# First norms with tokens on partitions and spread through a diagonal, constant products ahead of them, division and second root moved

## The chip, the cores and the metric

The kernel runs on 1 core of one Trainium2 chip. The metric is the device time of one execution in microseconds (us), lower is better. Runs of the kernel before took 2447.05, 2449.82 and 2451.08 us; the median is 2449.82 us.

The core has five engines with queues of their own, each in order: TensorE (PE; its weight loads are shown apart as PEld), VectorE (DVE), ScalarE (ACT), GpSimd (POOL) and SyncE (SP). In this kernel SP's queue issues most transfers, and POOL's queue issues those that add to what lies at their target.

## What is computed

One conditioned transformer block, with x added once more. Everything is float32.

```python
def _tc_rmsnorm(x, t, gw, gb, bw, bb):
    g = (t @ gw.T + gb)[:, None, :]
    b = (t @ bw.T + bb)[:, None, :]
    inv_rms = jax.lax.rsqrt(jnp.mean(x * x, axis=-1, keepdims=True) + EPS)
    return g * x * inv_rms + b

def _attention(x, Wq, Wk, Wv, Wo):
    ...
    attn = jnp.einsum('blhd,bmhd->bhlm', q, k) / scale
    p = jax.nn.softmax(attn, axis=-1)
    o = jnp.einsum('bhlm,bmhd->blhd', p, v).reshape(B, L, D)
    return o @ Wo.T

def _swiglu(x, gate_w, hid_w, out_w):
    return jax.nn.silu(x @ gate_w.T) * (x @ hid_w.T) @ out_w.T

y = x + _attention(_tc_rmsnorm(x, t, g1w, g1b, b1w, b1b), Wq, Wk, Wv, Wo)
y = y + _swiglu(_tc_rmsnorm(y, t, g2w, g2b, b2w, b2b), gate_w, hid_w, out_w)
return x + y
```

x is 4 x 1024 x 512, the condition t 4 x 128; there are 16 heads of 32, and the hidden width is 2048. EPS is 1e-6.

## The kernel before

**Layout and tiles.** Features lie on the 128 partitions, tokens along the free dimension: a tile of x is 128 x 4 x 512 (4 chunks of features, 512 tokens, a "block"). There are 8 blocks, two for each batch. The mean over features in a norm is therefore a product with a matrix `ones_mean` of 1/512 on PE, which also spreads the mean over all partitions.

**Start (L707 to L738).** The tiles y[0, 0] and y[0, 1] of the first batch are loaded and normed ahead of the loop. `norm_sum` (L210) squares four chunks on ACT, adds them up by four products with `ones_mean`, takes the root on ACT (L218) and the reciprocal on DVE (L219), both on 128 x 512. `norm_rest` (L222) scales each chunk on DVE (L199) and applies g and b on ACT (L202). `modulation` (L718) computes g and b by 16 narrow products (L722). Then come the first projections to keys, queries and values.

**The loop (L774).** One step g is one round of attention scores for 4 heads, 256 queries and 256 keys. Four steps make a group j (kind = g % 4 is the place in it), 32 steps make a block of tokens, and there are 256 rounds. A step computes `scores` on PE and copies them out on ACT (`keep`, L323); `running_max` follows on DVE; one group later `shifted` (L369) subtracts the maximum on DVE, ACT takes the exponential (L372), and `weighted` (L382) multiplies by v on PE a step after that. `accumulate` (L396) adds up the exponentials by transfers from POOL's queue, and `fold_sum`, `sums` and `sums_out` bring a group's sum of exponentials to the tile `total`, three groups after its scores, at kind 0. `inverse` (L422) and `normalize` (L431) divide the group's output by it on DVE: a reciprocal and a product on 128 x 256. Between `max_T` (L337) and `shifted`, the maximum goes through `parts` (DVE), `parts_T` (L353, transposes on PE into a PSUM tile pt at kind 1), a copy mT on ACT and two products `spread` (tiles sp) that ACT copies to `shift`.

**The feed-forward part.** From step FS = 60 on (`ffn`), the steps also carry the feed-forward products of the block before: an even and the following odd step share one p, a piece of 128 hidden features. The four half products use the tiles pa (`bank_a`) and pb; `filler` (L746) multiplies earlier pieces with the output weights into a tile pc, and `take_contract` (L583, "evict") adds pc to `res` on DVE. For p below 4 the filler is a late projection of values instead, and its eviction a copy on ACT. On an even step the order is: pair_26, copy_156, sums (kind 0), exponential, max_T and parts (kind 0), filler, running_max, evict, pair_7, sub_5 (L552), and at the end of the step the division of group j_n, where `in_first` places it at kind 0 or kind 2. On an odd step: pair_3, gate_tanh, exponential, pair_15 (next pa), take_5, then the gates.

**Order.** PE, DVE, ACT and POOL run in exactly the order in which the program issues instructions (`manual_schedule`, L704); work is hung on steps by four tables: `pinned` (near the start), `amid`, `halfway` and `ended` (the end of the step; `after` fills it). SP's transfers follow in their order too.

**PSUM.** Eight banks: four for scores (`ps_sc`), one for `av`, two of tag "w" in pool `ps`, one in `ps_b`. In the feed-forward stretch pb holds `ps_b`; pa, pc, pt, sp and the sums use tag "w". A tile waits for a bank until the last reader of an earlier tile there is done.

**Second norms (L648 to L676).** For block n, with e near the block's end: `norm_squares`, `norm_mean` (e + 17; product and a copy on ACT, L157), `norm_compact` writes one row of 512 means to DRAM, `take` reads it back as 128 x 4 (e + 19), `root` takes the root on ACT (e + 20, L173), `invert` the reciprocal on DVE (e + 21, L177), `put` writes it to DRAM (e + 22, L182), and `norm_spread` reads it back to all partitions (e + 24, one transfer, L188). For the first block the last three come one or two steps earlier. The norms of the later batches' inputs (`norm_root`, L149) stay on ACT and DVE with 128 x 512.

Of the kernel before, what the change touches and what calls it, by code (L numbers as in the profile page):

```python
# [9 lines left out]

F32 = mybir.dt.float32
BF16 = mybir.dt.bfloat16
AF = mybir.ActivationFunctionType
ALU = mybir.AluOpType
# [3 lines left out]
P = 128  # L18
NB = 512
# [5 lines left out]
def tile_cond_transformer_block(  # L25
# [13 lines left out]
    nc = tc.nc  # L39
    NBLK, _, C, _ = x.shape  # L40
    B = cond_t.shape[1]
    D = C * P
# [3 lines left out]
    KT = L // P  # L46
# [11 lines left out]
    sb = ctx.enter_context(tc.tile_pool(name="sb", bufs=1))  # L58
# [61 lines left out]
    state = {}  # L120
# [30 lines left out]
    def norm_mean(tag: str, inside: bool):  # L151
        if inside:
            pm = ps_av.tile([P, NB], F32, tag="av", name=f"pm{tag}")
        else:
            pm = ps.tile([P, NB], F32, tag="w", name=f"pm{tag}")
        mm(pm, ones_mean, state[tag], True, True)
        nc.scalar.copy(state[tag], pm)  # L157

    def compact(tag: str, t, rows: int, n: int):

# [3 lines left out]
    def take(tag: str):  # L164

        src = inv_s.pop(tag)
        few = sb.tile([P, src.shape[0] * src.shape[1] // P], F32, tag="few", name=f"few{tag}", bufs=2)
# [3 lines left out]
    def root(tag: str):  # L171
        few = state["few", tag]
        nc.scalar.activation(few, few, AF.Sqrt, bias=eps)  # L173

    def invert(tag: str):
        few = state["few", tag]
        nc.vector.reciprocal(few, few)  # L177

    def put(tag: str):
        few = state.pop(("few", tag))  # L180
# [28 lines left out]

    def norm_sum(dst, tag: str):  # L210

        pm = ps.tile([P, NB], F32, tag="w", name=f"pm{tag}")
        for c in range(C):
            sq = sb.tile([P, NB], F32, tag="h", name=f"sq{tag}_{c}", bufs=7)
            nc.scalar.activation(sq, dst[:, c, :], AF.Square)
            nc.tensor.matmul(pm, ones_mean, sq, start=(c == 0), stop=(c == C - 1))
        inv = sb.tile([P, NB], F32, tag="rmax" if tag == "a0_0" else "tot", name=f"inv{tag}", bufs=1)
        nc.scalar.activation(inv, pm, AF.Sqrt, bias=eps)  # L218
        nc.vector.reciprocal(inv, inv)  # L219
        state[tag] = inv  # L220

    def norm_rest(which: int, b: int, dst, tag: str):  # L222
        for c in range(C):
            norm_scale(dst, tag, c)
            norm_mod(which, b, dst, c)
# [99 lines left out]
    def running_max(r: int, k: int):  # L325
        j, u = divmod(r, UN)
        if u:
            nc.vector.tensor_tensor(rmax[j], rmax[j], raw[r][:, k, :, :], ALU.max)  # L328
        elif k:
            rmax[j] = sb.tile([P, HG, HQ], F32, tag="rmax", name=f"rmax{j}")  # L330
            nc.vector.tensor_tensor(rmax[j], raw[r][:, 0, :, :], raw[r][:, 1, :, :], ALU.max)
# [89 lines left out]
    def inverse(j: int):  # L421
        nc.vector.reciprocal(state["total", j], state["total", j])  # L422
# [183 lines left out]
    def after(g, fn, *a):  # L606
        ended.setdefault(g, []).append((fn, a))
# [40 lines left out]
    for n in range(NBLK):  # L648
        g0 = (n + 1) * BS
        pin(g0 + 6, load_res, n)  # L650
        e = g0 if n == 0 else g0 - 4
        go = e + 13 if n < NBLK - 1 else g0 + 8
        for d in range(C):
            first.append((go, None, project_out, (n, d)))
            pin(go - 3 + (d // 2 * 4 if n else 0), load_wo, n, d)
        if n < NBLK - 1:
            tag = f"f{n}"
            after(e + 16, add_res, n)
            for k in range(2):
                after(e + 15 + k, lambda n=n, tag=tag, k=k: norm_squares(x2[n], tag, k))  # L660
            if n == 0:
                between(e + 17, norm_mean, tag, False)
            else:
                amid.setdefault(e + 17, []).append((norm_mean, (tag, True)))
            after(e + 17, norm_compact, tag)
            after(e + 19, take, tag)
            after(e + 20, root, tag)
            after(e + (20 if n == 0 else 21), invert, tag)
            after(e + (21 if n == 0 else 22), put, tag)
            after(e + (22 if n == 0 else 24), norm_spread, tag)  # L670
            scales, mods = ((24, 24, 25, 25), (25, 25, 26, 26)) if n == 0 else ((22, 22, 24, 24), (23, 23, 25, 25))
# [32 lines left out]
    with tc.manual_schedule(  # L704
# [8 lines left out]
        load_modw(1)  # L713
        fetch()
        fetch()
        norm_sum(y[0, 0], "a0_0")

        def modulation(k: int):  # L718
            pm = ps.tile([P, 4 * C, B], F32, tag="w", name=f"pmod{k}")
            cols = slice(k * 2 * C, (k + 1) * 2 * C)  # L720
            for i in range(k * 2 * C, (k + 1) * 2 * C):
                nc.tensor.matmul(pm[:, i, :], modw[:, i * P : (i + 1) * P], condT, start=True, stop=True)  # L722
            nc.vector.tensor_tensor(
                mod[:, cols, :], pm[:, cols, :], modb[:, cols].unsqueeze(2).to_broadcast([P, 2 * C, B]), ALU.add
            )

        modulation(0)
        norm_rest(0, 0, y[0, 0], "a0_0")
        evicts = [project_kq(0, 0, which, 0) for which in range(2)]
        norm_sum(y[0, 1], "a0_1")  # L730
        for evict in evicts:
            evict()
        norm_rest(0, 0, y[0, 1], "a0_1")
        for kt in range(KT // 2):
            project_v(0, kt)()
            if kt == 0:
                modulation(1)
        project_kq(0, 0, 0, 1)()  # L738

# [34 lines left out]
        while g < END:  # L774
# [40 lines left out]
                keep(g)  # L815
            if kind == 1 and s_on:
                take_av(j_s)
            due = bool(first) and first[0][0] <= g
            if not ffn:
                if x_on:  # L820
# [24 lines left out]
            elif even:  # L845
# [13 lines left out]
                if g < NR:  # L859
                    running_max(g, 0)  # L860
                    running_max(g, 1)
                if evict is not None:
                    evict()
                pair_7(p)
# [3 lines left out]
            else:  # L868
# [143 lines left out]
```

## Time and profile before

| | |
|---|---|
| profiled execution | 2455.29 us |
| its span, first to last instruction | 2453.4 us |
| median of the runs | 2449.82 us |
| DVE / ACT / POOL busy | 1940.7 / 1413.2 / 172.4 us |
| mean granted clock of TensorE | 0.994 |
| L422 DVE reciprocal of total, 128x256 | x64, 1744 ns |
| L431 DVE product with it, 128x256 | x64, 425 ns |
| L583 DVE eviction of pc, 128x512 | x128, 689 ns |
| L173 ACT root, 128x4 | x7, 297 ns, with 7 table loads of 1283 ns |
| L177 DVE reciprocal, 128x4 | x7, 168 ns |
| L219 DVE reciprocal, 128x512 | x2, 3353 ns |
| PE waiting for L372 (exponential) ahead of L382 | 35.1 us, 37 times |

A line of the timeline reads: start in us, duration of the group in us, engine, line of the program, operation, target <- sources, shapes, count; in brackets the idle time of that engine ahead of it and what ended it. Groups of equal neighbours are merged, and matmuls overlap, so that a group of 16 can end after the next has begun. The granted clock (PEclk) is the share of TensorE's clock that was let through.

### The profile page before, as it was taken

How to read it: one execution, taken by the hardware profiler on the slowest of the kernel's cores; microseconds unless marked ns; L12 is line 12 of the kernel's file. 1: busy time of each engine (PE TensorE's matmuls, PEld its weight loads, DVE VectorE, ACT ScalarE, POOL GpSimd, SP SyncE). 2: the span in 40 equal slices, each digit the busy share in tenths (PEclk: the TensorE clock that was granted, in tenths of full speed). 3: DMA queues.
4: the chain of work that ended last, by engine and by line, in shares of the span. 5: the costliest groups of instructions: out<-in, count | busy, mean ns of one | idle time of the engine just before them, and what ended most of it. 6: DMA issues, size and time to landing. Idle time of an engine off the chain costs nothing. (4 is left out here: it accounts for less than half of the span.)

```text
span 2453.4 us, 72677 instructions
## 1 busy us (share of the span) xinstructions
PE 2385.5 (97%) x32553; PEld 1135.9 (46%) x32553; DVE 1940.7 (79%) x2183; ACT 1413.2 (58%) x1495; POOL 172.4 (7%) x207
## 2 busy tenths in 40 slices
PE   8999999999999999999999999999999999999999
PEld 3333334344444544544454544454445445444444
DVE  2688888878799988998899979997999799843332
ACT  3677776765566656665566656665666566512110
POOL 0000000000000000000000000000000000000000
PEclk9999999999999999999999999999999999999999
DMA  6599999988788788889888888898788888853442
GB/s 216 166 304 259 256 258 240 231 202 219 198 205 210 188 226 209 208 207 229 204 200 213 225 197 209 204 230 207 198 207 203 224 200 204 198 165 117 140 131 70
DMA packets 185988, 501.79 MB, mean 205 GB/s; under 512 B 21319, under 2 KB 78663, under 8 KB 158286
## 3 DMA queue, kind: packets, MB, share of 16 engines
q0 software_dynamic: 28656, 208.68, 43.9%
q1 hardware_dynamic: 156734, 288.47, 35.4%
q8 instruction: 256, 4.19, 0.7%
q14 instruction: 54, 0.44, 0.1%
q10 hardware_dynamic: 288, 0.01, 0.0%
HBM read 246.44 MB, written 41.97 MB: 118 GB/s over the span
## 5 line engine op out<-in xcount | busy, mean ns | idle before, releaser
L369 DVE TENSOR_TENSOR raw<-raw,shift 128x2048 f32<-128x2048 f32 (+1 forms) x320 | 588.8, 1857 | 25.6 <-ACT shift L364 25.6
L323 ACT COPY raw<-sc 128x2048 f32<-128x2048 f32 x256 | 479.7, 1874 | 187.4 <-PE sc L316 130.8
L372 ACT ACTIVATE raw<-raw 128x2048 f32<-128x2048 f32 x256 | 490.8, 1917 | 157.1 <-DVE raw L369 154.8
L328 DVE TENSOR_TENSOR rmax<-rmax,raw 128x1024 f32<-128x1024 f32 x384 | 469.5, 1223 | 48.8 <-ACT raw L323 42.2
L112 PE MATMUL pc<-h,ow 128*32 128x512 f32 x4096 | 470.5, 596 | 5.2 <-DMA ow<-in_out_w 4.2
L382 PE MATMUL av<-raw,v 128*32 128x256 f32 x4096 | 271.9, 383 | 35.6 <-ACT raw L372 35.1
L396 POOL DMA_DIRECT2D raw<-raw x192 | 165.3, 861 | 1967.4 <-ACT raw L372 878.9
L316 PE MATMUL sc<-q,k 32*128 32x256 f32 x4096 | 293.3, 400 | 1.0 <-ACT raw L323 1.0
L112 PE MATMUL pa<-x,fa 128*32 128x256 f32 x4096 | 272.5, 384 | 4.1 <-DVE pa L530 4.1
L112 PE MATMUL pa<-sums,fw 128*32 128x256 f32 x4096 | 271.5, 383 | 0.0
L112 PEld LDWEIGHTS pc<-h,ow 128*32 128x32 f32 x4096 | 128.6, 110 | 250.7 <-issue 231.9
L316 PEld LDWEIGHTS sc<-q,k 32*128 32x128 f32 x4096 | 184.9, 184 | 117.4 <-issue 75.8
L112 PE MATMUL pkq<-y,wkq 128*32 128x512 f32 (+1 forms) x1664 | 232.5, 594 | 4.3 <-ACT y L202 4.1
L112 PEld LDWEIGHTS pa<-x,fa 128*32 128x32 f32 x4096 | 124.7, 110 | 119.7 <-DVE pa L530 21.4
L382 PEld LDWEIGHTS av<-raw,v 128*32 128x32 f32 x4096 | 110.4, 109 | 149.4 <-ACT raw L372 66.0
L112 PEld LDWEIGHTS pa<-sums,fw 128*32 128x32 f32 x4096 | 134.4, 111 | 90.0 <-issue 3.4
L583 DVE SCALAR_TENSOR_TENSOR res<-pc,res 128x512 f32<-128x512 f32 x128 | 88.2, 689 | 78.9 <-PE pc L112 76.2
L545 ACT COPY pb<-pa 128x256 f32<-128x256 f32 x128 | 46.1, 360 | 174.4 <-PE pa L112 173.3
L562 ACT ACTIVATE t<-pa 128x512 f32<-128x512 f32 x128 | 78.1, 610 | 109.9 <-PE pa L112 109.6
L112 PE MATMUL pb<-x,fw 128*32 128x256 f32 x2048 | 134.0, 379 | 1.2 <-ACT pb L545 1.2
L112 PE MATMUL pa<-x,fw 128*32 128x256 f32 x2048 | 134.0, 379 | 0.0
L552 DVE TENSOR_TENSOR pb<-pb,p 128x256 f32<-128x256 f32 x128 | 55.0, 430 | 99.8 <-PE pb L112 94.2
(108 smaller groups left out, 2243.7 us busy)
## 6 DMA issues: line engine op xcount, KB each, us to landing
raw<-raw POOLq DMA_DIRECT2D x192, 1024.0 KB, 9.3
fw<-sw SPq DMA_DIRECT2D x128, 512.0 KB, 7.8
fa<-in_gh_w SPq DMA_DIRECT2D x128, 384.0 KB, 6.8
ow<-in_out_w SPq DMA_DIRECT2D x128, 256.0 KB, 3.1
wkq<-in_kq_w SPq DMA_DIRECT2D x32, 512.0 KB, 6.2
v<-vs SPq DMA_DIRECT2D x128, 128.0 KB, 6.6
k<-kqs SPq DMA_DIRECT2D x124, 128.0 KB, 6.5
kqs<-st SPq DMA_DIRECT2D x61, 256.0 KB, 8.3
```

The source lines that it names most:

```text
L112: nc.tensor.matmul(dst[k : k + n, :], w[:, k : k + n], moving, start=start, stop=stop, skip_group_check=seeded)
L316: nc.tensor.matmul(sc[:, i, k, :], keys[rows, k * P : (k + 1) * P], queries[rows, :], start=True, stop=True)
L323: nc.scalar.copy(raw[r].rearrange("p k h q -> p h k q"), state.pop(("sc", r)))
L328: nc.vector.tensor_tensor(rmax[j], rmax[j], raw[r][:, k, :, :], ALU.max)
L369: nc.vector.tensor_tensor(t, t, s.unsqueeze(1).to_broadcast(list(t.shape)), ALU.add)
L372: nc.scalar.activation(raw[r], raw[r], AF.Exp)
L382: nc.tensor.matmul(av[j][i * DH : (i + 1) * DH, :], v[m, u][:, k, i * DH : (i + 1) * DH], raw[r][:, k, i, :], start=(kt == 0), stop=(kt == ...
L396: nc.gpsimd.dma_start(out=acc[j].rearrange("p k h q -> p (k h q)"), in_=raw[r].rearrange("p k h q -> p (k h q)"), accum_op=ALU.add,)
L545: nc.scalar.copy(bank_b[p][:, RIGHT], bank_a[p][:, RIGHT])
L552: nc.vector.tensor_tensor(b[:, LEFT], b[:, RIGHT], fifth.pop(p), ALU.subtract)
L562: nc.scalar.activation(state["t", p], bank_a[p], AF.Tanh, scale=0.5)
L583: nc.vector.scalar_tensor_tensor(r, pp, 0.5, r, ALU.mult, ALU.add)
```

## The change

Four things are changed.

1. `norm_sum`, used twice at the start, adds the four squares on DVE, multiplies each 128 tokens of the sum (as weights) with one column of `ones_mean`, so that tokens lie on partitions, and takes root and reciprocal on 128 x 4. A diagonal 128 x 4 x 128 of these numbers, times 512, is built on DVE, and a later product of `ones_mean` with it spreads them over the partitions into a PSUM tile, from which the scaling reads. That product, `spread_root`, comes after `modulation(0)` for the first norm and after the first projection of values for the second; `modulation(1)` moves one projection later.
2. Eight products of `ones_mean` with itself stand ahead of the first norm.
3. In the second norms the mean gets eps on the way out of PSUM; root and reciprocal are replaced by `inverse_root`: one instruction on DVE that makes a first guess from the bits, and 17 on POOL (four Newton steps), at e + 21. For the first block `put` and `norm_spread` come one step later.
4. In the feed-forward stretch the division of a group moves from the end of the step to just ahead of the eviction. Before step 60 it stays at the end.

```diff
@@ norm_mean @@
-        nc.scalar.copy(state[tag], pm)
+        nc.scalar.activation(state[tag], pm, AF.Identity, bias=eps)
@@ root, invert @@
-        nc.scalar.activation(few, few, AF.Sqrt, bias=eps)
...
-        nc.vector.reciprocal(few, few)
+    def inverse_root(tag: str):
+        few = state["few", tag]
+        y, t = (sb.tile(list(few.shape), F32, tag=f"few{i}", name=f"few{i}{tag}") for i in range(2))
+        nc.vector.tensor_scalar(
+            y.bitcast(I32), few.bitcast(I32), 1, 0x3FFFFFFF, ALU.logical_shift_right, ALU.bitwise_xor
+        )
+        nc.gpsimd.tensor_scalar_mul(y, y, 1.35 * 2.0**62)
+        for _ in range(4):
+            nc.gpsimd.tensor_tensor(t, y, y, ALU.mult)
+            nc.gpsimd.tensor_tensor(t, t, few, ALU.mult)
+            nc.gpsimd.tensor_scalar(t, t, -0.5, 1.5, ALU.mult, ALU.add)
+            nc.gpsimd.tensor_tensor(y, y, t, ALU.mult)
+        state["few", tag] = y
@@ norm_sum @@
-        pm = ps.tile([P, NB], F32, tag="w", name=f"pm{tag}")
+        sq = [sb.tile([P, NB], F32, tag="h", name=f"sq{tag}_{c}", bufs=7) for c in range(C)]
         for c in range(C):
-            sq = sb.tile([P, NB], F32, tag="h", name=f"sq{tag}_{c}", bufs=7)
-            nc.scalar.activation(sq, dst[:, c, :], AF.Square)
-            nc.tensor.matmul(pm, ones_mean, sq, start=(c == 0), stop=(c == C - 1))
-        inv = sb.tile([P, NB], F32, tag="rmax" if tag == "a0_0" else "tot", name=f"inv{tag}", bufs=1)
-        nc.scalar.activation(inv, pm, AF.Sqrt, bias=eps)
-        nc.vector.reciprocal(inv, inv)
-        state[tag] = inv
+            nc.scalar.activation(sq[c], dst[:, c, :], AF.Square)
+            if c:
+                nc.vector.tensor_tensor(sq[0], sq[0], sq[c], ALU.add)
+        nt = NB // P
+        pm = ps.tile([P, nt], F32, tag="w", name=f"pm{tag}")
+        for t in range(nt):
+            nc.tensor.matmul(pm[:, t : t + 1], sq[0][:, t * P : (t + 1) * P], ones_mean[:, 0:1], start=True, stop=True)
+        few = sb.tile([P, nt], F32, tag="few", name=f"few{tag}")
+        nc.scalar.activation(few, pm, AF.Sqrt, bias=eps)
+        nc.vector.reciprocal(few, few)
+        diagonal = sb.tile([P, nt, P], F32, tag="t", name=f"diagonal{tag}", bufs=2)
+        nc.vector.scalar_tensor_tensor(
+            diagonal,
+            ident.unsqueeze(1).to_broadcast([P, nt, P]),
+            float(D),
+            few.unsqueeze(2).to_broadcast([P, nt, P]),
+            ALU.mult,
+            ALU.mult,
+        )
+
+        def spread_root():
+            inv = ps.tile([P, NB], F32, tag="w", name=f"inv{tag}")
+            nc.tensor.matmul(inv, ones_mean, diagonal.rearrange("p t q -> p (t q)"), start=True, stop=True)
+            state[tag] = inv
+
+        return spread_root
@@ second norms of a block @@
-            after(e + 20, root, tag)
-            after(e + (20 if n == 0 else 21), invert, tag)
-            after(e + (21 if n == 0 else 22), put, tag)
-            after(e + (22 if n == 0 else 24), norm_spread, tag)
+            after(e + 21, inverse_root, tag)
+            after(e + 22, put, tag)
+            after(e + (23 if n == 0 else 24), norm_spread, tag)
@@ start @@
-        norm_sum(y[0, 0], "a0_0")
+        ahead = ps.tile([P, P], F32, tag="w", name="ahead")
+        for _ in range(8):
+            nc.tensor.matmul(ahead, ones_mean, ones_mean, start=True, stop=True)
+        spread_root = norm_sum(y[0, 0], "a0_0")
...
         modulation(0)
+        spread_root()
         norm_rest(0, 0, y[0, 0], "a0_0")
         evicts = [project_kq(0, 0, which, 0) for which in range(2)]
-        norm_sum(y[0, 1], "a0_1")
+        spread_root = norm_sum(y[0, 1], "a0_1")
         for evict in evicts:
             evict()
+        project_v(0, 0)()
+        spread_root()
         norm_rest(0, 0, y[0, 1], "a0_1")
-        for kt in range(KT // 2):
+        for kt in range(1, KT // 2):
             project_v(0, kt)()
-            if kt == 0:
+            if kt == 1:
                 modulation(1)
@@ loop, even step of the feed-forward stretch @@
                 if g < NR:
                     running_max(g, 0)
                     running_max(g, 1)
+                divide()
                 if evict is not None:
                     evict()
                 pair_7(p)
@@ loop, end of a step @@
-            if n_on and j_n < direct and kind in (0, 2):
-                at = g - kind
-                in_first = j_n % GB == GB - 1 or (at >= FS and at % BS not in (12, 24, 28))
-                if in_first == (kind == 0):
-                    inverse(j_n)
-                    if j_n != GB:
-                        normalize(j_n)
+            if not ffn:
+                divide()
```

`divide` holds the same condition and the same two calls as the lines that are taken out at the end of the step. The tile `few` of `take` has one buffer instead of two.

More of the change, by code (lines that the diff above doesn't have):

```diff
@@ L11 @@
 F32 = mybir.dt.float32
+I32 = mybir.dt.int32
 BF16 = mybir.dt.bfloat16
@@ L166, in take @@
         src = inv_s.pop(tag)
-        few = sb.tile([P, src.shape[0] * src.shape[1] // P], F32, tag="few", name=f"few{tag}", bufs=2)
+        few = sb.tile([P, src.shape[0] * src.shape[1] // P], F32, tag="few", name=f"few{tag}")
         nc.sync.dma_start(out=few, in_=src.rearrange("h (p c) -> (h p) c", c=few.shape[1]))
         state["few", tag] = few
-    def root(tag: str):
+    def inverse_root(tag: str):
         few = state["few", tag]
-        nc.scalar.activation(few, few, AF.Sqrt, bias=eps)
-    def invert(tag: str):
-        few = state["few", tag]
-        nc.vector.reciprocal(few, few)
+        y, t = (sb.tile(list(few.shape), F32, tag=f"few{i}", name=f"few{i}{tag}") for i in range(2))
[9 more added lines that the diff above has]
+        state["few", tag] = y
     def put(tag: str):
@@ L817, in tile_cond_transformer_block, with divide @@
                 take_av(j_s)
+            def divide():
+                if n_on and j_n < direct and kind in (0, 2):
+                    at = g - kind
+                    in_first = j_n % GB == GB - 1 or (at >= FS and at % BS not in (12, 24, 28))
+                    if in_first == (kind == 0):
+                        inverse(j_n)
+                        if j_n != GB:
+                            normalize(j_n)
             due = bool(first) and first[0][0] <= g
```

## The prediction

> **What bounds the kernel now.** First the page's row of engines, then the waits, then timelines around each place that the diff touches.
>
> ```profile
> PE 2385.5 (97%) x32553; PEld 1135.9 (46%) x32553; DVE 1940.7 (79%) x2183; ACT 1413.2 (58%) x1495; POOL 172.4 (7%) x207
> ```
>
> TensorE is busy for 2385.5 of 2453.4 us: whatever makes it wait is paid nearly in full, and the other engines matter by what they make it wait for. Only 68 us of PE idleness are there to be won, and 5.49 of them lie ahead of its first product.
>
> The second view is the end of a step of kind 0 in the feed-forward stretch, on VectorE and then on TensorE.
>
> ```profile
> 706.84 1.22 DVE L331 TENSOR_TENSOR rmax<-raw 128x1024 f32<-128x1024 f32 x1
> 708.16 0.69 DVE L583 SCALAR_TENSOR_TENSOR res<-pc,res 128x512 f32<-128x512 f32 x1
> 709.09 0.43 DVE L552 TENSOR_TENSOR pb<-pb,p 128x256 f32<-128x256 f32 x1 [0.24 <-PE pb L112]
> 709.43 1.74 DVE L422 RECIPROCAL total<-total 128x256 f32<-128x256 f32 x1
> 711.21 0.43 DVE L431 TENSOR_TENSOR oT<-avs,total 128x256 f32<-128x256 f32 x1
> 711.55 2.35 DVE L369 TENSOR_TENSOR raw<-raw,shift 128x1024 f32<-128x1024 f32 x2
> ```
> ```profile
> 704.45 3.64 PE L112 MATMUL pc<-h,ow 128*32 128x512 f32 x32
> 707.91 1.05 PE L112 MATMUL pb<-x,fw 128*32 128x256 f32 x16
> 708.90 0.27 PE L353 MATMUL pt<-ident_bf,split 128*32 128x128 bf16 x2
> 709.10 1.15 PE L316 MATMUL sc<-q,k 32*128 32x256 f32 x16
> ```
>
> The eviction L583 ends at 708.85 and the transposes pt start at 708.90. This is no accident. The pool `ps` has two banks of tag "w". In this stretch one holds pa(p) until the gate in the next step; the sums, pc, pt, both sp and the next pa take turns in the other. So pt can't start until L583 has emptied pc's bank, and scores, spread and all that follows stand behind pt on PE. I looked at every step of kind 0 after which a division now comes: pt starts 0.05 us after that eviction's end in all of them (739.95 after 739.89, 863.07 after 863.02). That margin is nil.
>
> Third, ScalarE and TensorE two steps later.
>
> ```profile
> 706.92 1.28 ACT L173 ACT_TABLE_LOAD   x1
> 708.22 0.30 ACT L173 ACTIVATE fewf<-fewf,eps 128x4 f32<-128x4 f32 x1
> ...
> 714.42 1.28 ACT L372 ACT_TABLE_LOAD   x1
> ```
> ```profile
> 717.68 1.07 PE L382 MATMUL av<-raw,v 128*32 128x256 f32 x16 [1.39 <-ACT raw L372]
> ```
>
> The small root L173 costs two table loads, and the second delays the exponential that PE then waits for.
>
> **The division moved (50 times, in the feed-forward stretch alone).** Reciprocal 1.74 plus product 0.43 are 2.17 us that now stand ahead of the eviction. The rule of `in_first` puts the division at kind 0 where the group's place in its 32 steps is 0, 4, 8, 16 or 20, else at kind 2.
>
> Kind 0: L331 ends at 708.06, so the eviction would start at 710.23 instead of 708.16: 2.07 later. pt follows it, and so do scores, mT, spread and shift; VectorE, done with its division, waits for the shift. Nothing downstream had slack that this uses up, so I count it whole. At places 4, 8 and 20 VectorE idled 0.41 us for pc ahead of L583, which the division fills: 2.17 - 0.41 = 1.76. There are 11 groups at 0 and 16 (22.8 us), 17 at 4, 8 and 20 (five or six of each; some idle less, 1.77 on average, 30.1 us) and a last one at step 256, without a running maximum, at 0.95. Step 64 is free (ScalarE evicts there), step 68 too (PE waits 4.2 us for ow, longer than the division). Sum **+53.8**. Bounds: 0, if pt had a bank of its own, which the 0.05 us speak against, and 29 x 2.17 = 63.
>
> Kind 2: no transposes follow, and pa comes 2.4 to 2.9 us after the eviction. At place 26 alone it is 1.83, so pa slips by 0.47, ahead of a wait of 1.57 that swallows it. Elsewhere the division fills idle gaps of 0.10 and 0.24 around L583, so that the next shift, exponential and weighted product come 0.34 earlier; twelve waits of PE of 0.27 and 0.20 lie there. I take 12 x 0.34 = **-4** (bounds 0 and -6).
>
> **The clock.** A PE that waits can lose clock. After six equal waits of 1.57 us at place 28, the granted clock was 0.50 for 3.41 us four times, as here, and 1.00 twice:
>
> ```profile
> core 0: us, PE busy (x), PEclk, DMA share, GB/s
> 793.57:796.98 3.41, 3.41 (x36) 0.50 1.08 316
> 1312.40:1315.80 3.40, 2.96 (x44) 1.00 1.10 294
> ```
>
> After waits of 1.39 it never was. That step took 13.65 us against 12.60 without, so one costs 1.05; the most is half of 3.41, 1.71. I cut the trace's matmul starts into windows of 3.41 us: the half-clock stretches inside the kernel follow windows in which nothing streamed for 1.9 us or more. With the new waits put in, and averaged over the phase, some 19 windows are such, against 5 now. 14 more at 1.4 are **+20** (bounds 0 and 29 x 1.71 = 50).
>
> The Trainium skill (TensorE: Matmul & The Clock Gate, section HAM oscillation) names idle gaps above about 3.4 us as what throttles. By that rule the new waits would cost no clock, and the sum would end 20 us lower; the 1.57 us waits of this trace disagree with it, and the rows decide.
>
> **The second norms' root (seven times).** Gone from ScalarE: two loads of 1.28 and a root of 0.30; from VectorE a reciprocal of 0.17. The waits of PE behind them are 1.39 six times and 1.45 once (at 480.78): **-9.8** (bounds 0 and -7 x 2.86 = -20). Added: one VectorE instruction on 128x4 (0.17, as that reciprocal) and 17 on GpSimd. No row has GpSimd arithmetic that small; its memset of 128x1 took 0.10, its select of 128x128 0.28, so 1.7 to 4.8 in all; I take 3. GpSimd idled 12.37 us ahead of its accumulating transfer at 724.41, which hides most of it; that transfer may come 1 us late, in a chain that the fold reads several steps later. `put` on SP's queue then waits until some 723 instead of 720.0. Behind it stand v (720.43), the spread and ow (723.97), read three, two and two steps later, at 5.5 to 10 us a step: cost 0. For the first block `put` and its spread move by one step; the scaling then follows one step of 10.6 us after the spread: 0 as well. Were the cover gone, 7 x 4.8 = 34 at worst. The copy with eps as a bias costs as L149 does, 0.69 for 0.62, on an engine that is 58% busy: 0.
>
> The Trainium skill (ScalarE: Activation LUTs, section What ACT_TABLE_LOAD costs) adds a drain to each load, 2.66 us a switch. By that figure ScalarE would win 7 x 5.6 = 39 us, and were all of it on PE's path the sum would be 29 lower; the rows show 1.28 with no gap around it, and 1.39 on PE.
>
> **The first norms.** Now:
>
> ```profile
> 5.49 5.17 PE L216 MATMUL pma<-sqa,ones_mean 128*128 128x512 f32 x8 [5.49 <-ACT sqa L215]
> 10.51 1.84 PE L722 MATMUL pmod<-condT,modw 128*128 128x4 f32 x16
> 16.41 1.22 PE L112 MATMUL pkq<-y,wkq 128*128 128x512 f32 x1 [4.05 <-ACT y L202]
> ```
>
> A root (0.69) and a reciprocal (3.35) on 128x512 lie ahead of the scaling. After: squares end at 7.67; the last of three sums (0.69) at 8.4; eight narrow passes (1.84 / 16 = 0.115 each) 0.9; root 0.30; reciprocal 0.17; diagonal 0.69 (as L567); with hand-overs 11.1. But pmod stands ahead of the spreading product on PE until 12.35. Then two passes (0.43 each, 0.85 at half clock), a scaling of 0.69, a modulation of 0.82: the projections start at 14.9 to 15.8 instead of 16.41. I take -1.2. In the second norm eight passes of 0.43 and a wait of 0.78 go; eight of 0.115 and two of 0.43 come: -2.4. Together **-3.6**. The eight constant products, 16 passes of 0.11 to 0.21, lie in PE's first 5.49 us, where it waits for x: 0, and 3.4 if they ran into the sums. What they do to the clock is open: it was at 0.52 from 16.41 to 22.35, worth 2.9 us, which may go or come twice. Bounds of the part: -7 and +2.
>
> **Sum.** 53.8 - 4 + 20 - 9.8 - 3.6 = +56.4. The profiled execution took 2455.29 (span 2453.4), 5.5 above the median of the runs, 2449.82; the sum on it is 2511.7, on the median **2506**.
>
> **Rivals.** (1) The wait without the clock: nothing throttles, since the new waits differ from that at place 28 in what surrounds them. Then +36, 2486; against it stand four cases in six. (2) The clock drops at nearly every wait: 53.8 + 50 - 17.4 = +86, 2536. For it: transposes, scores and spread, which use the array thinly, surround each new wait. (3) Faster: pt finds an empty bank, because the slots are given out otherwise than I read them. Then only the gains are left, -17.4, and the filled gaps at kind 0 give nothing, as the shift sets that end: 2432. It decides where pt starts before L583 ends; each pair shown above speaks against it. (4) The wait holds, but VectorE's lead from the early division comes back in the same group: about half of 53.8 stays, with 10 of clock, +20, 2470. Against: pt delays the shift, which VectorE needs next.
>
> **How the numbers follow.** Forecast 0.62, (1) 0.12, (2) 0.08, (4) 0.08, (3) 0.08, and 0.02 that gains and waits cancel. A measurement here tells about 0.2% (5 us) from no change. Slower: 0.90; within: 0.02; faster: 0.08. The range, 2474 to 2536, takes in (1), (2) at its end and most of the bounds of the unknowns; (3) and part of (4) lie below it.
>
> **What would show it.** The transposes L353 with a wait of 1.7 to 2.1 us put down to VectorE in five groups of each block of 32 steps, pt 0.05 after L583, and L583 directly behind L431. Some 20 stretches of half clock, a mean clock near 0.985 instead of 0.994. No table load beside an exponential in the feed-forward stretch, and no 1.39 left. Step 0's scores at 46 to 48 us instead of 50.54. I am wrong if pt starts unhindered, if the gaps close without a change of the span, or if SP's queue, held by `put`, makes PE wait for ow.

## The result and the profile after

The changed kernel took 2518.15, 2518.72, 2522.99 and 2527.08 us, median 2520.85; the kernel before, on the same chip, 2450.45 (2449.82 without one execution of 3478.25 us that stands outside the ratio). The ratio, over the runs and not of the medians, is 1.0296 with a 95% interval of 1.0268 to 1.0324: slower, and inside the predicted range of 2474 to 2536, 15 us above the predicted 2506. The profiled execution is the one of 2518.15 (span 2516.4, mean clock 0.996), against 2455.29 (span 2453.4, clock 0.994) before: 63.0 us more of span.

First the page's row of engines, then the waits of TensorE (line waited on, what released it, us in total, times, longest).

```profile
PE 2393.3 (95%) x32573; PEld 1139.7 (45%) x32573; DVE 1936.3 (77%) x2191; ACT 1393.3 (55%) x1474; POOL 265.9 (11%) x326
```
```profile
PE pt L381 <- DVE res L611: 48.1, 29, 1.9
PE av L410 <- ACT raw L400: 27.5, 32, 1.6
PE pb L113 <- ACT pb L573: 21.2, 7, 4.8
```

TensorE is busy for only 7.8 us more than before, so most of the 63 is waiting. The first wait is new, 29 times, and is the one that the prediction is built on. The third stood at 1.2 us, once, before; now it is 21.2 in seven. And POOL is busy for 265.9 us where it was 172.4: 93.5 more, for 119 instructions that had been put at 0.10 to 0.28 each, 12 to 33 in all.

The place of each microsecond comes from a comparison of the two traces: the start of the scores of every step before and after, and the growth of each step, added up over blocks 2 to 7 by the step's place in its 32 (place 0 to 31).

| Where | Growth, us | What is there |
|---|---|---|
| up to step 0 | -2.1 | first norms (48.47 instead of 50.54) |
| blocks 0 and 1 | -1.6 | a table load's wait gone (1.45) |
| places 0, 8, 16, 20 | +9.2, +9.7, +8.9, +9.7 | wait of pt |
| place 4 | +2.8 | five steps longer by 1.62, for waits of pt of 1.57; the sixth, without a wait of pt, 5.3 shorter: its wait for ow is 2.5 shorter, with less half clock behind it |
| places 1 and 17 | +4.8 | half clock behind a wait of pt |
| place 18 | -8.5 | waits behind a table load gone |
| places 22, 23, 24 | +26.5, +4.4, +4.1 | wait of pb |
| places 27 and 28 | +2.2, -6.4 | four half-clock stretches of before gone |
| tail, after the last scores | -1.0 | |

The rows add up to 62.7. Two causes make nearly all of it: some 45 us for the transposes, where 53.8 and some clock were predicted, and 35 us in steps 22 to 24, which the prediction costed at nothing.

**The wait of pt** on VectorE and TensorE of the changed kernel (start, duration, engine, line, operation, target and sources; idle time before in brackets).

```profile
729.86 1.22 DVE L359 TENSOR_TENSOR rmax<-raw 128x1024 f32<-128x1024 f32 x1
731.00 1.74 DVE L450 RECIPROCAL total<-total 128x256 f32<-128x256 f32 x1
732.78 0.42 DVE L459 TENSOR_TENSOR oT<-avs,total 128x256 f32<-128x256 f32 x1
733.12 0.68 DVE L611 SCALAR_TENSOR_TENSOR res<-pc,res 128x512 f32<-128x512 f32 x1
733.72 0.42 DVE L580 TENSOR_TENSOR pb<-pb,p 128x256 f32<-128x256 f32 x1
```
```profile
727.78 3.64 PE L113 MATMUL pc<-h,ow 128*32 128x512 f32 x32
731.24 1.05 PE L113 MATMUL pb<-x,fw 128*32 128x256 f32 x16
733.85 0.27 PE L381 MATMUL pt<-ident_bf,split 128*32 128x128 bf16 x2 [1.57 <-DVE res L611]
734.06 1.15 PE L344 MATMUL sc<-q,k 32*128 32x256 f32 x16
```

The eviction (now L611) stands directly behind the division and ends at 733.80; pt starts at 733.85, again 0.05 later. Its wait is 1.57 at places 4, 8 and 20 (17 times), 1.88 at 0 and 16 (11 times) and 0.74 in the last group.

**The chain on GpSimd**, and VectorE beside it.

```profile
703.03 0.86 POOL L424 DMA_DIRECT2D raw<-raw  x1 [8.30 <-DMA raw<-raw]
712.37 2.18 POOL L179 TENSOR_SCALAR few0f<-few0f 128x4 f32<-128x4 f32 x1 [8.47 <-DVE few0f L176]
714.63 1.03 POOL L181 TENSOR_TENSOR few1f<-few0f 128x4 f32<-128x4 f32 x1
715.74 1.19 POOL L182 TENSOR_TENSOR few1f<-few1f,fewf 128x4 f32<-128x4 f32 x1
717.01 0.20 POOL L183 TENSOR_SCALAR few1f<-few1f 128x4 f32<-128x4 f32 x1
717.29 0.20 POOL L184 TENSOR_TENSOR few0f<-few0f,few1f 128x4 f32<-128x4 f32 x1
717.57 0.20 POOL L181 TENSOR_TENSOR few1f<-few0f 128x4 f32<-128x4 f32 x1
717.84 2.21 POOL L182 TENSOR_TENSOR few1f<-few1f,fewf 128x4 f32<-128x4 f32 x1
...
727.48 0.20 POOL L184 TENSOR_TENSOR few0f<-few0f,few1f 128x4 f32<-128x4 f32 x1
727.98 0.90 POOL L424 DMA_DIRECT2D raw<-raw  x1 [0.31 <-issue]
738.98 0.88 POOL L424 DMA_DIRECT2D raw<-raw  x1 [10.10 <-issue]
```
```profile
712.18 2.29 DVE L397 TENSOR_TENSOR raw<-raw,shift 128x2048 f32<-128x2048 f32 x1
714.38 2.48 DVE L356 TENSOR_TENSOR rmax<-rmax,raw 128x1024 f32<-128x1024 f32 x2
716.78 0.69 DVE L611 SCALAR_TENSOR_TENSOR res<-pc,res 128x512 f32<-128x512 f32 x1
717.38 0.42 DVE L580 TENSOR_TENSOR pb<-pb,p 128x256 f32<-128x256 f32 x1
717.71 2.28 DVE L397 TENSOR_TENSOR raw<-raw,shift 128x2048 f32<-128x2048 f32 x1
```

One form of instruction, 128x4, takes 0.20 us or up to 2.21. The chain of 17 lasts 15.3 us from 712.37 to 727.68 (so in six of the seven chains; 10.6 in the first). Set the ends side by side: POOL's 2.18 ends at 714.55, VectorE's shift at 714.47; 1.19 ends at 716.93, the second running maximum at 716.86; 2.21 ends at 720.05, the next shift at 719.99. All 53 of the 119 that take over 0.25 us end 0.05 to 0.09 us after a VectorE instruction that reads two inputs from SBUF (shift, running maximum, fold, once the product L459). Those beside L611 and L580, which read PSUM, or beside the one-input reciprocal stay at 0.20. So, as the records lie, a small GpSimd instruction waits out such a VectorE instruction. The Trainium skill (GPSIMD Engine Reference, table of section 1, row SBUF interfaces) says that GpSimd's are shared with VectorE, in contention with instructions that have two SBUF inputs; the records agree, and add how long it can be (2.21 us).

Behind the chain, on POOL's queue, stands the accumulating transfer L424. It was due at about 716.5, goes out at 727.98, and the next at 738.98. ScalarE and TensorE show who needs them:

```profile
741.94 0.62 ACT L590 ACTIVATE t<-pa 128x512 f32<-128x512 f32 x1
750.70 1.87 ACT L351 COPY raw<-sc 128x2048 f32<-128x2048 f32 x1 [8.14 <-DMA raw<-raw]
752.47 0.38 ACT L573 COPY pb<-pa 128x256 f32<-128x256 f32 x1
```
```profile
752.90 1.49 PE L113 MATMUL pb<-x,fw 128*32 128x256 f32 x16 [4.81 <-ACT pb L573]
754.31 2.09 PE L344 MATMUL sc<-q,k 32*128 32x256 f32 x16
```

ScalarE's copy of the next scores needs a buffer of the ring of raw tiles, which comes free when the transfer lands; it idles 8.14 us. The copy L573 stands behind it in ScalarE's queue, and TensorE waits 4.81 us for that, four steps after the chain. Scores that take 1.15 us then take 2.09, at half clock.

**The start**, on TensorE:

```profile
1.04 3.78 PE L746 MATMUL ahead<-ones_mean 128*128 128x128 f32 x16 [1.04 <-DVE eps L75]
8.38 1.87 PE L229 MATMUL pma<-ones_mean,sqa 128*128 128x1 f32 x8 [3.56 <-DVE pick L83]
10.11 3.55 PE L753 MATMUL pmod<-condT,modw 128*128 128x4 f32 x16
13.52 2.06 PE L245 MATMUL inva<-diagonala,ones_mean 128*128 128x512 f32 x2
```

The modulation's 16 passes take 3.55 us where they took 1.84, and the eight narrow passes 1.87, against 0.95 in the second norm: everything ahead of the scaling runs at half speed. The first projections begin at 17.20, not 16.41. The constant products end 3.56 us before the first narrow pass.

### The profile page after: what moved, and what is told of

It is laid out like the page before. It is cut to its first block, busy times and chain, and to the rows that moved or that the text cites. A ratio compares the mean times of both kernels' runs of the same rounds, so it can differ in the third digit from the quotient of the medians.

```text
span 2516.4 us, 72809 instructions
## 1 busy us (share of the span) xinstructions
PE 2393.3 (95%) x32573; PEld 1139.7 (45%) x32573; DVE 1936.3 (77%) x2191; ACT 1393.3 (55%) x1474; POOL 265.9 (11%) x326
## 5 line engine op out<-in xcount | busy, mean ns | idle before, releaser
L397 DVE TENSOR_TENSOR raw<-raw,shift 128x2048 f32<-128x2048 f32 (+1 forms) x320 | 589.5, 1858 | 93.8 <-ACT shift L392 93.8
L356 DVE TENSOR_TENSOR rmax<-rmax,raw 128x1024 f32<-128x1024 f32 x384 | 469.6, 1223 | 88.7 <-ACT raw L351 82.2
L424 POOL DMA_DIRECT2D raw<-raw x192 | 165.6, 862 | 1868.2 <-ACT raw L400 760.5
L113 PE MATMUL pb<-x,fw 128*32 128x256 f32 x2048 | 134.6, 380 | 21.2 <-ACT pb L573 21.2
L383 ACT COPY mT<-pt 12x256 bf16<-12x256 bf16 x64 | 23.2, 362 | 216.3 <-PE pt L381 216.3
L573 ACT COPY pb<-pa 128x256 f32<-128x256 f32 x128 | 46.3, 361 | 165.8 <-PE pa L113 164.6
L611 DVE SCALAR_TENSOR_TENSOR res<-pc,res 128x512 f32<-128x512 f32 x128 | 87.9, 687 | 60.5 <-PE pc L113 59.0
```

The lines of the kernel that those rows point to most:

```text
L113: nc.tensor.matmul(dst[k : k + n, :], w[:, k : k + n], moving, start=start, stop=stop, skip_group_check=seeded)
L383: nc.scalar.copy(mT[j][:NP], pt[:NP, :, :].rearrange("p a b -> p (a b)"))
L397: nc.vector.tensor_tensor(t, t, s.unsqueeze(1).to_broadcast(list(t.shape)), ALU.add)
L424: nc.gpsimd.dma_start(out=acc[j].rearrange("p k h q -> p (k h q)"), in_=raw[r].rearrange("p k h q -> p (k h q)"), accum_op=ALU.add,)
L573: nc.scalar.copy(bank_b[p][:, RIGHT], bank_a[p][:, RIGHT])
L611: nc.vector.scalar_tensor_tensor(r, pp, 0.5, r, ALU.mult, ALU.add)
```

## The experiments

Medians, in us. The kernel before took 2450.47, 2450.52 and 2451.12 in the three sets below.

### The division: three places for it

`a_div_end`, the changed kernel with the division back at the end of the step:

```diff
-                divide()
                 if evict is not None:
...
-            if not ffn:
-                divide()
+            divide()
```

> The changed kernel with the division of the feed-forward stretch back at the end of the step; all else as changed. Theory (the division ahead of the eviction holds the bank that the transposes need, 48.1 us of PE waits in 29 places): those waits go, the 21.2 us of pb waiting for ScalarE stay, 2466 to 2480 us. Rival (the waits only show where a delay from elsewhere surfaces, so that it comes up at another place): above 2500 us.

`a_div_after_evict`, the changed kernel with the division one call later:

```diff
-                divide()
                 if evict is not None:
                     evict()
+                divide()
                 pair_7(p)
```

> The changed kernel with the division one place later, directly behind the eviction instead of ahead of it, still ahead of pair_7. Theory (it is the eviction's delay, by way of the bank, and nothing else of the move): the transposes start unhindered, the same 2466 to 2480 us as with the division at the end, possibly 3 us less, since idle gaps of VectorE are filled. Rival (the division early in the step hurts by itself, for instance through the subtraction behind it, L580, which then comes 2.2 us later): above 2495 us.

`b_div_only`, the kernel before with the division moved as in the change, and nothing else:

```diff
                     running_max(g, 1)
+                divide()
                 if evict is not None:
...
+            if not ffn:
+                divide()
```

> The kernel before with the division alone moved ahead of the eviction. Theory: the transposes wait 1.6 to 1.9 us in 29 places, 48 us in all, less a few us that kind 2 wins; 2492 to 2502 us. Rival (the loss needs the other parts of the change, such as GpSimd's chain): under 2470 us. Clock: some stretches of half clock more than before, each under 1 us in the total.

| Kernel | Median | Ratio to before, over the runs (95%) |
|---|---|---|
| a_div_end | 2481.25 | 1.0121 (1.0095 to 1.0147) |
| a_div_after_evict | 2478.15 | 1.0108 (1.0090 to 1.0126) |
| b_div_only | 2496.72 | 1.0180 (1.0158 to 1.0202) |

The wait of pt, 48.1 us in 29, is in `b_div_only` to the digit and in neither of the others. The division costs 46.2 us alone, and 40 to 43 within the change. That it need only stand one call later to cost nothing of this leaves one reason: what follows it, the eviction. `a_div_end` came out a little above its 2466 to 2480: what is left of the change costs 30.8 us (2481.25 against 2450.47), more than assumed there. Its waits of TensorE:

```profile
PE av L410 <- ACT raw L400: 32.1, 37, 1.6
PE pb L113 <- ACT pb L573: 23.6, 7, 4.6
PE sc L344 <- ACT raw L351: 8.4, 7, 1.7
```

### The bank of pt

`a_pt_bank` leaves the division early and gives pt a bank of the scores:

```diff
-        pt = ps.tile([P, HQ // P, P], BF16, tag="w", name=f"pt{j}")
+        pt = ps_sc.tile([P, HQ // P, P], BF16, tag="sc", name=f"pt{j}")
```

> The changed kernel with the PSUM tile pt of the transposes taken from the scores' banks instead of tag w. Theory (pt waits for the bank that the late eviction holds): pt no longer waits for VectorE; but the next scores now wait until ScalarE has copied pt, some 0.7 us at each of 64 groups, so that 48 us of waits become about 20 in the 29 groups and some 0.5 more in the others: 2490 to 2515 us. Rival (VectorE's order itself delays the group, whatever the bank): 2520 us or more with waits of the same size at another place, spread or shift.

2500.35 (1.0204, 1.0188 to 1.0220), 20.5 less than the changed kernel. The wait of pt is gone, with the eviction as late as ever; another, smaller one takes its place, since the scores now wait for pt's bank:

```profile
736.71 0.28 PE L381 MATMUL pt<-ident_bf,split 128*32 128x128 bf16 x2
737.44 1.15 PE L344 MATMUL sc<-q,k 32*128 32x256 f32 x16 [0.45 <-ACT mT L383]
```
```profile
PE sc L344 <- ACT mT L383: 28.5, 63, 0.6
```

48.1 against 28.5 us of wait: it is the bank that ties pt to the eviction, and a bank of its own would have to be one that nothing else waits for.

### The second root: which engine, and whose queue

`a_root_back` is the changed kernel with root, inversion and copy as they were, at their old steps:

```diff
-        nc.scalar.activation(state[tag], pm, AF.Identity, bias=eps)
+        nc.scalar.copy(state[tag], pm)
...
-            after(e + 21, inverse_root, tag)
-            after(e + 22, put, tag)
-            after(e + (23 if n == 0 else 24), norm_spread, tag)
+            after(e + 20, root, tag)
+            after(e + (20 if n == 0 else 21), invert, tag)
+            after(e + (21 if n == 0 else 22), put, tag)
+            after(e + (22 if n == 0 else 24), norm_spread, tag)
```

> The changed kernel with the second norms' root back on ScalarE and VectorE, at its old steps. Theory (GpSimd's 17 instructions take 15.3 us, hold back the accumulating transfers, and ScalarE's copy of the scores waits for their buffers): the 21.2 us of pb waiting for ScalarE go, waits of up to 1.4 us behind the table loads come back (at most 9.8 us in all); 2505 to 2513 us. Rival (the new wait of pb comes from the division's delay, not from GpSimd): it stays, and the time is 2525 us or more.

2490.11 (1.0156, 1.0138 to 1.0174): 30.7 less than the changed kernel, and below the 2505 to 2513 expected. That expectation took the 21.2 us of pb's wait for the whole price. The growth of places 22 to 24, 35.0, holds besides it the half clock behind the wait and the catching up of ScalarE; and this profile's clock is 0.999.

`b_root_pool` is the kernel before with the new root alone, `b_root_dve` the same with its 17 instructions on VectorE:

```diff
-        nc.gpsimd.tensor_scalar_mul(y, y, 1.35 * 2.0**62)
+        nc.vector.tensor_scalar_mul(y, y, 1.35 * 2.0**62)
         for _ in range(4):
-            nc.gpsimd.tensor_tensor(t, y, y, ALU.mult)
+            nc.vector.tensor_tensor(t, y, y, ALU.mult)
...
```

> The kernel before with the second norms' root alone moved to GpSimd (first guess on VectorE, 17 small instructions on GpSimd, put and spread at their new steps). Theory (the chain lasts 15.3 us, since each of its instructions waits out a VectorE instruction with both inputs in SBUF; the accumulating transfers behind it come late and the ring of raw buffers runs out): new waits of pb and of the scores for ScalarE, 25 to 31 us; 2472 to 2484 us. Rival (the chain hurts only together with the moved division): 2438 to 2452 us, a gain by the table loads saved.

> As b_root_pool, but with the same 17 instructions on VectorE. Theory (the loss lies in GpSimd's chain and not in leaving ScalarE's root): 17 times some 0.17 us are 2.9 us on VectorE, SP's put goes out about as before, no wait of pb, the 1.39 us waits behind the table loads gone: 2438 to 2456 us. Rival (the later put and spread are what hurts): they still come, 2465 us or more.

On GpSimd 2484.51 (1.0136, 1.0118 to 1.0154), 0.5 above the expected 2472 to 2484, with 20.1 us of pb's wait; on VectorE 2454.47 (1.0018, 1.0009 to 1.0028), with none. The 17 take 3.4 us there, 0.20 from start to start. So the arithmetic isn't dear, its engine is. It isn't free either: place 18 wins the 8.49 us of the table loads in both, and on VectorE places 19 and 20 give back 10.7 and 2.6, as the shift and the exponential stand behind the 17:

```profile
722.24 1.07 PE L390 MATMUL av<-raw,v 128*32 128x256 f32 x16 [1.71 <-ACT raw L380]
```

`b_idle_chain` asks whose queue carries the delay, POOL's or SP's. It is the kernel before, its root untouched, with 17 GpSimd instructions that nobody reads:

```diff
+    def idle_chain(tag: str):
+        few = state["few", tag]
+        y, t = (sb.tile(list(few.shape), F32, tag=f"few{i}", name=f"few{i}{tag}") for i in range(2))
+        nc.gpsimd.tensor_scalar_mul(y, few, 1.0)
+        for _ in range(4):
+            nc.gpsimd.tensor_tensor(t, y, y, ALU.mult)
...
+            after(e + 21, idle_chain, tag)
```

> The kernel before, with root and reciprocal where they were and put unchanged, and beside them 17 instructions of the same kinds on GpSimd whose result nothing reads. Theory (GpSimd's own queue is what is held up, its accumulating transfers): the waits of pb for ScalarE come up although SP waits for nothing new, and the 1.39 us waits stay; 2474 to 2492 us. Rival (SP's queue, which stands 18.3 us at put, loads too late): no new wait, 2447 to 2455 us.

2482.94 (1.0130, 1.0108 to 1.0153). TensorE's wait, ScalarE's copy in front of it, and SP's wait ahead of `put`:

```profile
PE pb L112 <- ACT pb L555: 17.4, 7, 3.5
```
```profile
754.97 1.86 ACT L333 COPY raw<-sc 128x2048 f32<-128x2048 f32 x1 [6.80 <-DMA raw<-raw]
```
```profile
SPq L192 <- DVE fewf L177: 27.9, 7, 4.3
```

SP waits 27.9 us, as before the change to the digit; in the changed kernel it was 120.0 for the same transfer. Still 17.4 us of pb's wait are there. So the result of the chain, `put` and what SP has behind it aren't needed for the loss; the instructions on POOL are. Nor do they slow VectorE itself: its shift on 128x2048 takes 2.28 us and its running maximum 1.22, as before.

### The start

`b_start_only` is the kernel before with the first norms and the constant products of the change, `b_start_no_ahead` the same without these:

```diff
-        ahead = ps.tile([P, P], F32, tag="w", name="ahead")
-        for _ in range(8):
-            nc.tensor.matmul(ahead, ones_mean, ones_mean, start=True, stop=True)
         spread_root = norm_sum(y[0, 0], "a0_0")
```

> The kernel before with the first norms and the eight constant products of the change alone. Theory (the first norm's projections start no earlier, since the tensor clock is down when they come, and the second norm saves about 2.5 us of products): the scores of step 0 start at 47 to 49 us instead of 50.5, 2444 to 2450 us. Rival (the start is hidden behind loads that the loop waits for anyway): 2449 to 2452 us.

> b_start_only without the eight constant products. Theory (they end 3.6 us before the first product of the norm, so that the clock is lost again): step 0 within 1 us of b_start_only and the same time within 0.1%. Rival (they do raise the clock for the projections): step 0 later by 2 us or more, and the time with it.

2447.51 (0.9988, 0.9979 to 0.9998) and 2448.57 (0.9989, 0.9981 to 0.9998), against 2451.12: 3.6 and 2.6 us won, each with an interval of about 0.5 to 5 us. Scores of step 0 start at 47.62 and 47.32, the modulation takes 3.55 us in both. The constant products do nothing that could be measured.

### A version from the parts

`start_root_fused` is the start of the change, with the second root on VectorE in 11 instructions: the guess, its scaling, and three Newton steps instead of four, each of three instructions. The division stays where it was before. `start_root_fused_div` puts it directly behind the eviction as well.

```diff
-        for _ in range(4):
-            nc.gpsimd.tensor_tensor(t, y, y, ALU.mult)
-            nc.gpsimd.tensor_tensor(t, t, few, ALU.mult)
-            nc.gpsimd.tensor_scalar(t, t, -0.5, 1.5, ALU.mult, ALU.add)
-            nc.gpsimd.tensor_tensor(y, y, t, ALU.mult)
+        for _ in range(3):
+            nc.vector.scalar_tensor_tensor(t, y, -0.5, y, ALU.mult, ALU.mult)
+            nc.vector.tensor_tensor(t, t, few, ALU.mult)
+            nc.vector.scalar_tensor_tensor(y, t, 1.5, y, ALU.add, ALU.mult)
```

> b_start_only with the second norms' root on VectorE in 11 small instructions (three Newton steps of three instructions) instead of ScalarE's root. Theory (17 instructions there cost VectorE 2.9 us and PE 1.7 us at the next exponential, as much as the table loads had cost): 1.9 us of VectorE leave PE about 0.7 us of wait for 1.39 saved, six times: 4 us less than b_start_only, 2440 to 2446 us. Rival (another wait stands close behind the one removed): within 1 us of b_start_only.

> start_root_fused with the division directly behind the eviction in the feed-forward stretch, instead of the end of the step. Theory (behind the eviction it holds no bank and fills VectorE's idle 0.24 us ahead of the subtraction): 0 to 3 us less than start_root_fused. Rival (the subtraction is late for the products behind it): 2 us or more above it.

2444.26 (0.9970, 0.9958 to 0.9982) and 2435.31 (0.9947, 0.9926 to 0.9967). With 11 instructions places 19 and 20 give back 2.2 and 2.6 us instead of 10.7 and 2.6, and 8.49 are still won at 18. The last is the fastest kernel measured, 0.5% below the one before. How the division behind the eviction brings 9 us more, where 0 to 3 were expected, is only partly traced: blocks 2 to 7 are 3.0 us shorter, 2.0 of them at place 16; the other 5.6 lie in the tail, 4.2 of them as one wait of the last sums in the other's profile, which nothing ties to the edit.

## Why the prediction was right, and where it was wrong

| Step of the prediction | Predicted | Measured |
|---|---|---|
| division, kind 0 | +53.8 | 48.1 of waits; 45.6 of growth at places 0, 4, 8, 16 and 20 (five steps at place 4), the next row already taken off |
| division, kind 2 | -4 | about -2.7, at place 16 (six steps grew by 1.48 instead of 1.93) |
| clock | +20 | about 0 net in the profiled run: 4.8 behind pt, 4.2 gone at place 28 |
| second root: table loads gone | -9.8 | 8.5 + 1.45 |
| second root: chain on GpSimd | 0 | +35 |
| first norms | -3.6 | -2.1 at step 0 here; -3.6 on the medians of `b_start_only` (-0.5 to -5.1) |

**Right: the eviction, the bank, pt.** The 0.05 us between eviction and pt before the change was the whole argument, and it holds: pt follows by 0.05 after the change, waits 29 times, 11, 17 and one of them as counted, and steps 64 and 68 were free. `b_div_only` shows the price alone (46.2), `a_div_after_evict` that the eviction behind it carries it, `a_pt_bank` that the bank does. The size was some 10 to 15% high, because neighbours on VectorE overlap. The reciprocal starts 0.08 before the running maximum ends (731.00 and 731.08), the product 0.42 long is followed after 0.34; from start to start the division takes 2.12. Less these 0.08 and the 0.10 that VectorE idled ahead of the eviction before, that is 1.94, and a step at place 0 grew by 1.93, not 2.07. The waits are 1.88, 1.57 and 0.74 for 2.07, 1.77 and 0.95. Rival 3, an empty bank, and rival 4, half of it recovered, fall with this.

**Wrong: "its memset of 128x1 took 0.10, its select of 128x128 0.28, so 1.7 to 4.8 in all; I take 3."** That was the mis-sized term: the chain took 15.3 us. Rows of a GpSimd that worked alone were taken as the price of one that works beside VectorE, which is 77% busy, more than half of that with instructions that hold it off (shift 589.5 us, running maximum 469.6). With 3 us, "GpSimd idled 12.37 us ahead of its accumulating transfer" was cover enough, and that transfer "may come 1 us late, in a chain that the fold reads several steps later"; it came 11.5 late, and the nearer reader was not the fold but ScalarE's copy, through the ring of raw tiles. "7 x 4.8 = 34 at worst" is near the 35 measured, by accident: it counts chains of 4.8 in full, where chains of 15.3 come through in part. And the queue named as the danger was the wrong one: SP's `put` did wait (120.0 us for 27.9), while `b_idle_chain` loses 32.4 us with SP as before.

**Wrong: the clock, "14 more at 1.4 are +20".** The profiled execution has six half-clock stretches inside the kernel, as many as before (five or six); three follow waits of pt, three waits of pb. One of each:

```profile
core 0: us, PE busy (x) PEld busy (x) DVE busy (x) ACT busy (x) POOL busy (x), PEclk, DMA share, GB/s
753.40:756.80 3.40, 3.40 (x36) 1.56 (x32) 3.37 (x6) 1.61 (x2) 0.86 (x1) 0.50 0.95 193
...
975.00:978.40 3.40, 3.40 (x41) 1.87 (x44) 0.39 (x2) 0.95 (x2) 0.07 (x1) 0.54 0.95 193
```

Of the waits of pt, three of the eleven at 1.88 are followed by half clock, and none of the seventeen at 1.57. The four stretches at place 28 went away, where TensorE's wait of 1.57 became 1.20. So a wait of 1.57 cost clock four times in six at place 28 before, and never here: what a wait costs in clock couldn't be carried from the one place to the other.

The records of all fourteen profiles show what it depends on. The granted clock changes on a grid of 3.41 us. Between 60 and 2130 us, look at each window of that grid that is itself at full clock: with 1.0 to 1.7 us without a matmul by the records, none of 250 was followed by half clock; with 1.7 to 2.1, 29 of 58; with more, all 29. Two windows of the changed kernel, each with the one that follows, around a wait of 1.88 and one of 1.57:

```profile
core 0: us, PE busy (x), PEclk, DMA share, GB/s
971.87:975.28 3.41, 1.52 (x27) 1.00 0.37 91
975.28:978.69 3.41, 3.41 (x40) 0.50 0.95 192
1139.12:1142.53 3.41, 1.84 (x34) 1.00 1.00 241
1142.53:1145.94 3.41, 3.41 (x72) 1.00 1.02 288
```

A wait of 1.57 alone stays under 1.7; at place 28 before, a wait of 0.20 for pa lay in the same window and made it 1.77 in the four cases that lost clock. A wait of 1.88 counts only where it falls whole into one window. The prediction counted such windows too, averaged over where they fall, and with waits of 2.07 and 1.76, which lie above 1.7; so part of the +20 came with their size; this last is argued, as no run varied the length.

The other runs say the same of the division: `b_div_only` had clocks of 0.995 to 0.998 and `a_root_back` of 0.997 to 0.999, the kernel before beside them 0.994 to 0.998. They are lower where the chain stands on GpSimd: 0.991 to 0.993 in `b_root_pool`, whose profile has half clock at place 22 of all six blocks, 0.990 to 0.998 in `b_idle_chain`, and 0.996, 0.994, 0.992 and 0.986 in the changed kernel, with 2518.15, 2518.72, 2522.99 and 2527.08 us. So up to 9 us of a run are clock, and they go with pb's waits of up to 4.8 us more than with pt's. Rival 1, the wait without the clock, is what that profile shows for this part, and rival 2 is out.

**Errors against each other.** The total is 6.5 us off on the profiled executions (+62.9 against +56.4). For the chain 35 came that weren't forecast, and the start and kind 2 won some 3 less. Against that, 19 of clock didn't come, pt took nearly 6 less, and some 6 fell away that no term speaks of: 5.3 at place 4, by a wait for ow that differs from profile to profile (4.2 us before, 1.7 after, 2.2 in `a_div_end`), and 1.0 in the tail. On the medians it is 15: the profiled execution before lay 5.5 above the median of its runs, the one after 2.7 below. That the time fell into the range is owed in part to this, and so to luck: with the 20 of clock as well, the 2518.15 would have been 2538, past the range's end at 2536.

**The start: a sum near the forecast, from wrong parts.** The first norm was to win 1.2 and lost 0.8, as its narrow products and the modulation ran at half speed; the second was to win 2.4 and must have won about 3. Of the constant products the prediction said "What they do to the clock is open", which was fair; no effect could be measured.

**The table loads** went as said: -8.5 and -1.45, and no wait of 1.39 is left.

## What to carry to other kernels

Before work is put ahead of an instruction that empties a PSUM bank, look how close behind its end the next user of that bank starts: 0.05 us meant that the whole of the division was paid, and one call later it was not. Small arithmetic on GpSimd beside a VectorE that streams from SBUF took here the time of VectorE's instructions, not its own, and it held every transfer that GpSimd's queue issued behind it; look for the ring of buffers that those transfers free. When a forecast total fits, compare its terms with the trace all the same.

## What the runs showed of the hardware that was not expected

- A 128x4 instruction on GpSimd takes 0.20 us, or ends 0.05 to 0.09 us after the running VectorE instruction with two SBUF inputs: up to 2.21 us (53 of 119). VectorE's own instructions got no longer (2.28 us for the shift on 128x2048). This rests on how the records lie; no run varied VectorE's instruction by itself.
- The same on VectorE took 0.16 to 0.17, 0.20 from start to start: a dependent chain of 17 in 3.4 us.
- 16 constant passes over 3.78 us, then 3.56 us without a product, left TensorE at half speed: 16 narrow passes in 3.55 us with them and without them.
- The granted clock went by windows of 3.41 us on a grid, and not by the length of a wait: after a window with under 1.7 us without a matmul it was never halved (0 of 250 with 1.0 to 1.7), after 1.7 to 2.1 in 29 of 58, after more in 29 of 29. So waits of 1.57 at place 28 were followed by half clock four times in six, and waits of 1.57 for pt in none of 17.
